# Exact bfloat16 parts for one matrix product, scan states summed on GpSimd, gates by tanh, and filler products of constants on TensorE

## The chip, the core and the metric

The kernel runs on one core of a Trainium2 chip. A core has five engines that each work through their own queue of instructions in order: TensorE (matrix products; PE in the profile, with its weight loads as PEld), VectorE (DVE), ScalarE (ACT), GpSimd (POOL) and SyncE (SP, which issues DMAs here). The metric is the time of one execution on the device in microseconds (us), as the median of several runs.

## The reference, cut to what matters

There are 128 batches of 32 latent rows of 256 numbers, and for each batch a context of 257 rows. Everything is float32. For each batch the reference computes, in this order:

- layer norm, then cross attention of the latents over the raw context, with folded weights, added to the latents;
- a selective scan (a state space block). After a layer norm the rows are projected to 512 channels `x` and 512 channels `delta = relu(...)`. For each of 16 states `s`, `h_t = h_(t-1) * exp(A_s * delta_t) + x_t * delta_t` runs over the 32 rows of a batch; the output of a channel is `sum over s of w_s * h_s`, plus `x * D`, and it is multiplied by a gate, `sigmoid(W_gate * rows + b)`, before the output projection;
- a ternary MLP. `W_fc` holds only -1, 0 and 1: layer norm, 256 to 1024 with gelu, layer norm, 1024 to 256;
- linear attention over the context, whose keys and values are projected by the kernel (relu, cube, norms);
- self attention with a distance decay, 16 heads, over the 32 rows of a batch;
- an MLP with quantized weights and activations.

## The kernel before, in words

Four batches make a group: 128 rows, one row for each partition. There are 32 groups, joined into nine blocks of 2, 4, 4, 4, 4, 4, 4, 4 and 2 groups (`BLOCKS`, line 1442). For each group `context_group` (line 954) loads and transposes the context, does the cross attention, and projects keys and values (`keys`, `keys_values`, products `pkey` and `pval`). For each block `scan_block` (line 1115) does the scan, with the channels in four chunks of 128 partitions and all rows of the block along the free dimension (512 for four groups, 256 for two). For each group `latent_group` (line 1409) then does `mlp` (1171), `linear` (1196), `attention` (1247) and `quantized_mlp` (1379), and stores the rows.

None of this is issued where it is written. A `Recorder` (line 267) takes down every operation with what it reads and writes. `order` (line 384) then puts them in one order, by list scheduling: an estimate of each instruction's duration (`ns_of`, line 42), fixed delays after it (`TAIL`, `HOP`, lines 95 and 96), a due time for each operation that is interpolated within a span of its group (`DUE`, line 1445, one span for each call of `begin`), and constants that weigh the engines against each other (`PRICE`, `WINDOW`, `SOONER`, `AHEAD`, `HORIZON`, lines 554 to 558). It also chooses the engine where an operation may run on two, as `R.relu` and `R.copy` may. `trace` (line 533) issues them; each engine's queue keeps that order strictly. Because all recorded operations are issued by line 540, every row of the profile says L540, and rows are told apart by the names of their tiles.

Buffers are rings: `t1` and `t2` (lines 655 and 658) for intermediate tiles in SBUF, and `bank` (line 578) for the eight PSUM banks.

The places that the change touches:

- `scan_block`. The gate `yg` is a Sigmoid on ScalarE (line 1134). For each chunk, `acc` in PSUM starts as `x * D` (line 1143). For each of 16 states there is an Exp on ScalarE giving `a` (line 1151), a scan on VectorE giving `h` (line 1155), and on VectorE `acc = h * w + acc` (line 1158). Then `acc` is multiplied by the gate (line 1161).
- `mlp`. The rows are transposed by TensorE as they are; the weights `w_fc`, float32, are centred over their inputs once at the start (`centred`, called at line 897), which does the layer norm's subtraction; two halves `ph` of 512 columns are each two float32 products (line 1182).
- `attention`. The latent projection `plat` (line 1260) has its own bank, as has the value projection `pva` (line 1305), which comes after the scores' Exp.

Of the kernel before, what the change touches and what calls it, by code (L numbers as in the profile page):

```python
# [8 lines left out]
F32 = mybir.dt.float32  # L9
# [85 lines left out]
TAIL = {"vector": 75, "scalar": 100, "gpsimd": 25, "tensor": 130, "sync": 0}  # L95
HOP = {"vector": 38, "scalar": 38, "gpsimd": 80, "tensor": 55, "sync": 100}
TABLES = {AF.Exp: "exp", AF.Gelu: "gelu", AF.Sigmoid: "sigmoid"}
# [169 lines left out]
class Recorder:  # L267
# [8 lines left out]
    def together(self):  # L276

        recorder = self

        class Joined:  # L280
            def __enter__(self):
                recorder.joined = []

            def __exit__(self, *_):
                parts, recorder.joined = recorder.joined, None
                ways = {"tensor": ([c for p in parts for c in p[0]], sum(p[1] for p in parts), False)}
                recorder.add(ways, [r for p in parts for r in p[2]], [w for p in parts for w in p[3]])

        return Joined()

    def copy(self, out, in_):
        self.record({"scalar": ("copy", (out, in_), {}), "vector": ("tensor_copy", (out, in_), {})})

# [12 lines left out]
    def begin(self, stage):  # L306

        self.stage = stage
        self.group += 1
        self.spans[self.group] = DUE[self.group]  # L310

    def record(self, calls):
# [33 lines left out]
        if self.joined is not None:  # L346
            self.joined.append((*ways["tensor"][:2], reads, writes))
            return
# [35 lines left out]
    def order(self):  # L384
# [78 lines left out]
        while len(placed) < len(ops):  # L463
# [29 lines left out]
            for k in op.ways:  # L493
                ready[k].remove(i)
            ns = op.ways[e][1]
# [36 lines left out]

    def trace(self, tc):

        last = {}
        for i in self.order():
            op = self.ops[i]
            engine = getattr(self.nc, op.engine)
            for name, args, kw in op.ways[op.engine][0]:
                ins = getattr(engine, name)(  # L540
                    *(traced(a) for a in args), **{k: traced(v) for k, v in kw.items()}
                ).ins
                if op.engine in last:
                    tc.add_manual_dep(
                        ins, last[op.engine].name,
                        mybir.DependencyInfo(
                            mybir.DependencyClass.NoSync, mybir.DependencyReason.DATA
                        ),
                        reason="order",
                    )  # L550
                last[op.engine] = ins


PRICE = {"tensor": 0.0, "vector": 3.195, "scalar": 3.454, "gpsimd": 8.58, "sync": 0.0}
WINDOW = 31.919
SOONER = -0.015
AHEAD = 0
HORIZON = 0.832
# [3 lines left out]
def perceiver_kernel(ctx: ExitStack, tc: tile.TileContext, t: dict, out: bass.AP):  # L562
# [34 lines left out]
    nc.vector.tensor_copy(onesb, ones)  # L597

# [56 lines left out]
    def t2k(shape, name, dtype=F32):  # L655
        return ring("t2", 15).tile(shape, name, dtype)
# [51 lines left out]
    w_fc = wts.tile([P, 2, HID], F32, name="w_fc")  # L708
# [135 lines left out]
    def late_setup():  # L844
        R.vector.tensor_tensor(bd_in, b_in[:, 0:4], d_vec, ALU.mult)
# [51 lines left out]
        centred(w_fc, 2)  # L897
# [142 lines left out]


# [73 lines left out]
    def scan_block(x):  # L1115
        size = len(x)
        tok, batches = size * P, size * GB
# [13 lines left out]
        for ic in range(4):  # L1131
            pg = project(w_gate, ic * P)
            yg.append(t2k([P, TOK], "yg")[:, 0:tok])
            R.scalar.activation(yg[ic], pg, AF.Sigmoid, bias=b_gate[:, ic : ic + 1])
        for ic in range(4):

            dl = t2k([P, TOK], "dl")[:, 0:tok]
            R.scalar.activation(
                dl, project(w_in, DI + ic * P), AF.Relu, bias=b_in[:, 4 + ic : 5 + ic]
            )  # L1140
            xd = project(w_in, ic * P)
            acc = bank("acc")[:, 0:tok]
            R.scalar.activation(
                acc, xd, AF.Identity, bias=bd_in[:, ic : ic + 1], scale=d_vec[:, ic : ic + 1]
            )
            R.vector.scalar_tensor_tensor(xd, xd, b_in[:, ic : ic + 1], dl, ALU.add, ALU.mult)
            dv = dl.rearrange("p (b q) -> p b q", q=LQ)
            for s in range(NST):

                a = a_ring[s % NA][:, 0:batches, :]  # L1150
                R.scalar.activation(
                    a[:, :, 1:LQ], dv[:, :, 1:LQ], AF.Exp, scale=a_neg[:, ic, s : s + 1]
                )
                h = t2k([P, TOK], "h")[:, 0:tok]
                R.vector.tensor_tensor_scan(
                    h, a.rearrange("p b q -> p (b q)"), xd, 0.0, ALU.mult, ALU.add
                )
                R.vector.scalar_tensor_tensor(
                    acc, h, w_st[:, ic, s : s + 1], acc, ALU.mult, ALU.add
                )  # L1160
            R.vector.tensor_tensor(yg[ic], acc, yg[ic], ALU.mult)
# [9 lines left out]
    def mlp(xg):  # L1171

        _, r = stats(xg)
        xT = rows_T(xg)
# [3 lines left out]
        for k in range(2):  # L1178
            ph = bank("ph")
            cols = slice(k * 512, (k + 1) * 512)  # L1180
            with R.together():
                accumulate(ph, [(xT[:, dc, :], w_fc[:, dc, cols]) for dc in range(2)])
            R.scalar.activation(hid[:, cols], ph, AF.Gelu, scale=r)
            R.vector.bn_stats(st[:, k, :], hid[:, cols])
# [62 lines left out]
    def attention(xg):  # L1247
# [3 lines left out]
        with R.together():  # L1251
            for c in range(2):
# [3 lines left out]
                )  # L1256
        qT = t1k([P, D], "qTa").rearrange("p (c n) -> p c n", c=2)
        R.scalar.copy(qT, pq[:, 0:D].rearrange("p (c n) -> p c n", c=2))

        pl_ = bank("plat")  # L1260
        with R.together():
            accumulate(pl_[0:LAT, 0:P], [(wkd[:, dc], xT[:, dc, :]) for dc in range(2)])
        lat = t1k([P, P], "lat")[0:LAT]
        R.scalar.copy(lat, pl_[0:LAT, 0:P])

        pk = bank("pka")
        with R.together():
            for c in range(2):
                accumulate(pk[:, c * P : (c + 1) * P], [(wupk[:, c * P : (c + 1) * P], lat)])
        kd = t2k([P, 2, GB, 2, LQ], "kd")  # L1270
        for r in range(2):
# [3 lines left out]
                scale=odd[:, r : r + 1],  # L1275
            )
# [25 lines left out]

        vd = vds[turn[0] % NV]
        turn[0] += 1
        pv = bank("pva")
        with R.together():
            for b in range(GB):
                for r in range(4):
                    R.tensor.matmul(
                        pv[r * LQ : (r + 1) * LQ, b * 64 : (b + 1) * 64],  # L1310
                        lat[:, b * LQ : (b + 1) * LQ],
                        wupv.rearrange("p (j h k) -> p h j k", h=4, k=16)[:, r],
                        start=True, stop=True,
                    )
        for r in range(4):
            rows_ = slice(r * LQ, (r + 1) * LQ)
            R.scalar.copy(
                vd[rows_, :, :, r, 0:16],
                pv[rows_, 0 : GB * 64].rearrange("p (b j n) -> p b j n", b=GB, j=4),
            )  # L1320
# [88 lines left out]
    def latent_group(xg, kvc, rows_out):  # L1409
        mlp(xg)  # L1410
        linear(xg, kvc)
        attention(xg)
        quantized_mlp(xg)
# [4 lines left out]
    for i, size in enumerate(BLOCKS):  # L1418
# [12 lines left out]
        scan_block(x)  # L1431
# [8 lines left out]
NV = 2  # L1440
PAIR = 2
# [4 lines left out]
    (-1.0, -0.9), (-0.011, 0.566), (-0.809, -0.789), (-0.212, 0.821), (-0.767, 0.109),  # L1446
    (-0.01, 0.15), (0.299, 1.222), (0.556, 1.717), (1.591, 2.698), (1.87, 3.034), (0.619, 0.719),
    (0.863, 0.989), (1.148, 1.233), (1.17, 1.732), (1.498, 2.663), (2.591, 3.75425),
    (2.699, 3.86225), (2.806, 3.97), (2.915, 4.07825), (1.618, 1.802), (1.854, 2.163),
    (2.11, 2.23), (2.365, 2.485), (2.459, 3.663), (3.593, 4.75425), (3.7, 4.86225),  # L1450
    (3.807, 4.97025), (3.915, 5.07825), (2.571, 2.704), (2.985, 3.032), (3.115, 3.236),
    (3.365, 3.485), (3.5, 4.663), (4.591, 5.75425), (4.699, 5.86225), (4.807, 5.97025),
    (4.915, 6.07825), (3.61, 3.735), (3.864, 3.99), (4.115, 4.235), (4.365, 4.431), (4.5, 5.663),
    (5.591, 6.755), (5.699, 6.86225), (5.807, 6.97025), (5.915, 7.113), (4.615, 4.733),
    (4.866, 5.033), (5.115, 5.235), (5.365, 5.485), (5.5, 6.663), (6.612, 7.776), (6.72, 7.884),
    (6.7, 8.26), (6.921, 8.145), (5.616, 5.733), (5.924, 6.173), (6.117, 6.235), (6.462, 6.482),
    (6.501, 7.654), (7.288, 8.301), (7.441, 8.497), (7.544, 8.812), (7.594, 8.984),
    (6.632, 6.743), (6.921, 6.941), (7.171, 7.295), (7.361, 7.611), (7.495, 8.077),
    (7.815, 9.377), (7.667, 9.18), (7.008, 8.283), (7.34, 8.982), (7.658, 7.783), (7.829, 7.849),
    (8.0, 8.585), (8.023, 9.464), (8.392, 9.052),  # L1460
# [78 lines left out]
```

## Time and profile before

| | |
|---|---|
| median of 3 runs | 1765.29 us (1763.37 to 1765.42) |
| the profiled execution | 1760.93 us, of which the span from first to last instruction is 1759.2 us |
| mean granted TensorE clock | 0.973 of full speed |
| TensorE matmul busy | 1660.5 us |
| TensorE weight load busy (beside the products) | 1211.7 us |
| VectorE busy | 1554.4 us |
| ScalarE busy | 1430.8 us |
| GpSimd busy | 1117.0 us |
| table loads on ScalarE | 114, of 1283 ns each |

A row of the profile's groups reads: line, engine, operation, output tile<-input tiles, the shapes, how many; then the busy time of the group in us and the mean duration of one in ns; then the time that the engine stood idle just before them and what ended it. Durations of neighbouring instructions on an engine overlap at their ends, so the busy time of a group is less than count times mean; busy times count a moment once. A float32 matrix product is recorded as two instructions, a bfloat16 product or a transpose as one.

### The profile page before, as it was taken

The page shows a single profiled execution, that of the slowest core. Times are in us where ns is not written, and L with a number is a line of the kernel's source. Part 1 is how long each engine was busy: PE and PEld are TensorE (multiplying, and loading weights), DVE is VectorE, ACT ScalarE, POOL GpSimd, SP SyncE. Part 2 cuts the span into 40 slices and gives each one's busy share as a digit, 9 for nine tenths or more (in the row PEclk, how much of TensorE's full clock was granted, in tenths as well). Part 3 has the DMA queues.
Part 4 walks back from the last instruction along what each step waited for, and adds up shares of the span by engine and source line. Part 5 has one row for each costly group of instructions (what it writes and reads, how often), then busy time and mean ns, then how long its engine had stood idle before and what let it go on. Part 6 is the DMA issues. An engine that isn't in the chain of part 4 may idle for free.

```text
span 1759.2 us, 44923 instructions
## 1 busy us (share of the span) xinstructions
PE 1660.5 (94%) x17268; PEld 1211.7 (69%) x17299; DVE 1554.4 (88%) x3083; ACT 1430.8 (81%) x3442; POOL 1117.0 (63%) x1827
## 2 busy tenths in 40 slices
PE   8999999999999999999999999999999989597886
PEld 6787667766776777766776767766776667366564
DVE  3599799999898999899899999979999999999865
ACT  4587888888788997889788888889888898786655
POOL 5675556744776677666776747865776375347476
PEclk9999999999999999999999999999999999798886
DMA  7221101000110011001100021001100000000000
GB/s 243 74 83 47 61 29 32 29 31 4 48 42 2 16 59 35 29 2 40 41 29 29 7 65 37 29 2 40 40 29 29 1 8 20 4 4 5 5 4 22
DMA packets 44758, 59.69 MB, mean 34 GB/s; under 512 B 8704, under 2 KB 27008, under 8 KB 44544
## 3 DMA queue, kind: packets, MB, share of 16 engines
q1 hardware_dynamic: 44544, 56.81, 10.1%
q8 instruction: 137, 2.24, 0.5%
q14 instruction: 77, 0.63, 0.1%
HBM read 52.32 MB, written 4.19 MB: 32 GB/s over the span
## 4 chain that ended last, share of the span: by engine, by line
PE 75%; DVE 12%; ACT 7%; issue 1%; POOL 1%; DMA 0%; SPq 0%; DVEq 0%; ACTq 0%; POOLq 0%
PE pkey L540 13%; PE pval L540 11%; PE pproj L540 9%; PE pT L540 5%; PE pmlp L540 5%; DVE h L540 5%; PE ph L540 4%; PE pk L540 3%; PE pcT L540 3%; PE pout L540 3%; PE pq L540 3%; DVE acc L540 2%; PE psc L540 2%; PE pqa L540 2%; PE po L540 2%; PE pya L540 2%
## 5 line engine op out<-in xcount | busy, mean ns | idle before, releaser
L540 DVE TENSOR_TENSOR_SCAN h<-a,pproj 128x512 f32<-128x512 f32 (+1 forms) x576 | 617.4, 1087 | 12.4 <-ACT a L540 11.6
L540 ACT ACTIVATE a<-dl,a_neg 128x496 f32<-128x496 f32 (+1 forms) x576 | 369.8, 662 | 60.9 <-DVE h L540 57.6
L540 DVE SCALAR_TENSOR_TENSOR acc<-h,w_st,acc 128x512 f32<-128x512 f32 (+1 forms) x576 | 392.4, 681 | 0.1
L540 PE MATMUL pval<-wkv,cT 128*128 128x256 f32 x1024 | 245.7, 385 | 8.8 <-ACT hid L540 2.3
L540 PE MATMUL pkey<-wkv,cT 128*128 128x256 f32 x1024 | 238.1, 386 | 0.0
L540 POOL TENSOR_TENSOR ku<-ku,e 128x512 f32<-128x512 f32 x128 | 162.1, 1276 | 101.1 <-ACT ku L540 93.3
L540 PEld LDWEIGHTS pval<-wkv,cT 128*128 128x128 f32 x1024 | 189.6, 191 | 44.6 <-issue 7.4
L540 ACT ACTIVATE ks<-ku 128x256 f32<-128x256 f32 x512 | 208.1, 412 | 14.3 <-POOL ku L540 13.1
L540 PEld LDWEIGHTS pkey<-wkv,cT 128*128 128x128 f32 x1024 | 189.3, 190 | 37.7 <-issue 14.5
L540 POOL TENSOR_TENSOR ku<-ks,ku 128x512 f32<-128x512 f32 x128 | 163.7, 1285 | 29.8 <-ACT ks L540 29.1
L540 ACT ACT_TABLE_LOAD x114 | 146.3, 1283 | 5.1 <-PE ph L540 2.5
L540 POOL TENSOR_TENSOR kn<-kn,halves 128x4 f32<-128x4 f32 x128 | 134.1, 1048 | 22.5 <-ACT ks L540 21.7
L540 ACT ACTIVATE vf<-pval,kf 128x256 f32<-128x256 f32 x256 | 107.9, 471 | 40.0 <-PE pval L540 24.5
L540 POOL TENSOR_TENSOR rstd<-rstd,halves 128x1 f32<-128x1 f32 x224 | 123.7, 553 | 15.8
L540 POOL TENSOR_SCALAR rstd<-mv 128x1 f32<-128x1 f32 x224 | 42.9, 192 | 133.7 <-DVE mv L540 110.2
L540 PE MATMUL pproj<-xTs,w_in 128*128 128x512 f32 (+1 forms) x288 | 122.4, 552 | 0.5 <-ACT hT L540 0.2
L540 PE MATMUL ph<-w_fc,xT 128*128 128x512 f32 x256 | 120.2, 597 | 0.6 <-ACT xT L540 0.5
L540 PE MATMUL pmlp<-w_pr,hT 128*128 128x256 f32 x512 | 116.7, 381 | 1.5 <-ACT hT L540 1.2
L540 PEld LDWEIGHTS pmlp<-w_pr,hT 128*128 128x128 f32 x512 | 95.8, 190 | 20.7 <-issue 4.8
L540 ACT ACTIVATION_READ_ACCUMULATOR ks<-ku 128x1 f32 x512 | 99.4, 194 | 0.0
L540 ACT COPY cT<-pcT 128x512 f32<-128x512 f32 x128 | 71.8, 595 | 12.2 <-PE pcT L540 11.8
L540 DVE BATCH_NORM_STATS2 st<-x 128x6 f32<-128x256 f32 x192 | 78.7, 413 | 2.9 <-POOL x L540 1.7
(259 smaller groups left out, 3583.1 us busy)
## 6 DMA issues: line engine op xcount, KB each, us to landing
cx<-in_ctx_dram SPq DMA_DIRECT2D x64, 512.0 KB
x<-in_x_dram SPq DMA_DIRECT2D x32, 128.0 KB
cr<-in_ctx_dram SPq DMA_DIRECT2D x128, 32.0 KB
out_dram<-x SPq DMA_DIRECT2D x32, 128.0 KB
vlz<-vl SPq DMA_DIRECT2D x128, 1.1 KB
w_in<-in_w_inT_dram SPq DMA_DIRECT2D x1, 1024.0 KB
raw_fc<-in_w_fcT_dram SPq DMA_DIRECT2D x2, 512.0 KB
raw_pr<-in_w_prT_dram SPq DMA_DIRECT2D x2, 512.0 KB
```

Source lines behind the costliest of these rows:

```text
L540: ins = getattr(engine, name)(*(traced(a) for a in args), **{k: traced(v) for k, v in kw.items()}).ins
```

## The change

- `mlp`: the row's mean is subtracted first (`xc`, on VectorE or GpSimd as the planner chooses) and the result transposed to `xT`. `xT` is split into three bfloat16 parts `x3` that add up to it: round, subtract, round, subtract. `w_fc` is kept in bfloat16 (its values are -1, 0 and 1) and no longer centred. Each half `ph` is six bfloat16 products (three parts, two chunks of the contraction) in place of two float32 ones.
- `scan_block`: the first 2 states of each chunk (6 in the last two blocks) are multiplied by their weight and added on GpSimd, into a tile `some` in SBUF which starts as `x * D`. The later states go on in `acc` in PSUM on VectorE; the first of them reads `some`.
- The gate: `sigmoid(z) = 0.5 * (1 + tanh(z / 2))`. ScalarE computes tanh, which the planner counts as in the same table as Exp; VectorE computes `(yg + 1) * acc` in one instruction; the half is put into `w_out` at setup.
- `attention`: the latent projection shares the bank of `pqa`, the value projection that of `pka`, and the values are copied ahead of the scores.
- The planner: new `TAIL`, `PRICE` and the other constants, 251 due spans instead of 78 (with `part()`, stages have several), and `t2` has 17 buffers instead of 15.
- `keep_busy`: where the plan has TensorE idle for more than 600 ns ahead of a run that opens a float32 PSUM tile, products of two constant tiles (bfloat16, 512 columns) into that tile are issued first, one for each 216 ns of 0.7 of the gap less 200 ns. The real products then overwrite the tile. In the changed kernel as built there are 172 of them.

```diff
-TAIL = {"vector": 75, "scalar": 100, "gpsimd": 25, "tensor": 130, "sync": 0}
+TAIL = {"vector": 75, "scalar": 90, "gpsimd": 25, "tensor": 215, "sync": 0}
...
-TABLES = {AF.Exp: "exp", AF.Gelu: "gelu", AF.Sigmoid: "sigmoid"}
+TABLES = {AF.Exp: "exp", AF.Gelu: "gelu", AF.Tanh: "exp"}
...
+    def cast(self, out, in_):
+        self.record({
+            "scalar": ("copy", (out, in_), {}), "gpsimd": ("tensor_copy", (out, in_), {}),
+        })
+
+    def minus_column(self, out, in_, column):
+        wide = column.to_broadcast([P, size_of(in_)])
+        self.record({
+            "vector": ("tensor_scalar", (out, in_, column, None, ALU.subtract), {}),
+            "gpsimd": ("tensor_tensor", (out, in_, wide, ALU.subtract), {}),
+        })
...
+    def keep_busy(self, op):
+        out = op.ways["tensor"][0][0][1][0]
+        if min(out.buf.ops) != op.n or out.dtype != F32:
+            return
+        bank = out.buf.traced()[:, 0:512].rearrange("p (a b) -> p a b", a=4)
+        left, right = self.constants
+        for _ in range(int(FILL * (op.gap - 200.0) / 216.0)):
+            self.nc.tensor.matmul(
+                bank, left, right.unsqueeze(1).to_broadcast([P, 4, P]), start=True, stop=True
+            )
...
+            if op.engine == "tensor" and op.gap > GAP:
+                self.keep_busy(op)
...
-PRICE = {"tensor": 0.0, "vector": 3.195, "scalar": 3.454, "gpsimd": 8.58, "sync": 0.0}
-WINDOW = 31.919
-SOONER = -0.015
-AHEAD = 0
-HORIZON = 0.832
+GAP, FILL = 600.0, 0.7
+PRICE = {"tensor": 0.0, "vector": 20.786091, "scalar": 1.959533, "gpsimd": 3.101899, "sync": 0.0}
+WINDOW = 13.816
+SOONER = 0.066
+AHEAD = 0.777235
+HORIZON = 1.581593
...
-        return ring("t2", 15).tile(shape, name, dtype)
+        return ring("t2", 17).tile(shape, name, dtype)
...
-    w_fc = wts.tile([P, 2, HID], F32, name="w_fc")
+    w_fc = wts.tile([P, 2, HID], BF16, name="w_fc")
...
+        R.vector.tensor_scalar(b_gate, b_gate, 0.5, None, ALU.mult)
+        R.vector.tensor_scalar(w_out, w_out, 0.5, None, ALU.mult)
...
-        centred(w_fc, 2)
...
-            R.scalar.activation(yg[ic], pg, AF.Sigmoid, bias=b_gate[:, ic : ic + 1])
+            R.scalar.activation(yg[ic], pg, AF.Tanh, bias=b_gate[:, ic : ic + 1], scale=0.5)
...
-            acc = bank("acc")[:, 0:tok]
+            some = t2k([P, TOK], "some")[:, 0:tok]
...
-                R.vector.scalar_tensor_tensor(
-                    acc, h, w_st[:, ic, s : s + 1], acc, ALU.mult, ALU.add
-                )
-            R.vector.tensor_tensor(yg[ic], acc, yg[ic], ALU.mult)
+                weight = w_st[:, ic, s : s + 1]
+                if s < pooled:
+                    R.gpsimd.tensor_scalar(h, h, weight, 0.0, ALU.mult, ALU.add)
+                    R.gpsimd.tensor_tensor(some, some, h, ALU.add)
+                else:
+                    if s == pooled:
+                        acc = bank("acc")[:, 0:tok]
+                    R.vector.scalar_tensor_tensor(
+                        acc, h, weight, some if s == pooled else acc, ALU.mult, ALU.add
+                    )
+            R.vector.scalar_tensor_tensor(yg[ic], yg[ic], 1.0, acc, ALU.add, ALU.mult)
...
-        _, r = stats(xg)
-        xT = rows_T(xg)
+        mv, r = stats(xg)
+        xc = t1k([P, D], "xc")
+        R.minus_column(xc, xg, mv[:, 0:1])
+        xT = t1k([P, D], "xT")
+        transposed(xc, xT.rearrange("p (c n) -> p c n", c=2), 2)
+
+        x3 = t2k([P, 3, D], "x3", BF16)
+        R.cast(x3[:, 0, :], xT)
+        R.gpsimd.tensor_tensor(xT, xT, x3[:, 0, :], ALU.subtract)
+        R.cast(x3[:, 1, :], xT)
+        R.gpsimd.tensor_tensor(x3[:, 2, :], xT, x3[:, 1, :], ALU.subtract)
...
-                accumulate(ph, [(xT[:, dc, :], w_fc[:, dc, cols]) for dc in range(2)])
+                accumulate(ph, [
+                    (x3[:, k3, dc * P : (dc + 1) * P], w_fc[:, dc, cols])
+                    for dc in range(2) for k3 in range(3)
+                ])
...
+POOLED = 2
+LATE_POOLED = 6
```

## The prediction

> **What bounds the kernel now.** I read the busy time by engine first, then the same by stages, then the chain that ended last, then the groups of instructions.
>
> The stages, from the view of busy time by windows (us; after each busy time its instructions, then the granted clock, the DMA share, GB/s):
>
> ```profile
> core 0: us, PE busy (x) PEld busy (x) DVE busy (x) ACT busy (x) POOL busy (x), PEclk, DMA share, GB/s
> 0.00:100.00 100.00, 90.00 (x813) 69.80 (x814) 51.83 (x133) 52.57 (x168) 63.19 (x108) 0.98 0.48 155
> 100.00:1484.00 1384.00, 1355.35 (x14167) 990.45 (x14189) 1277.14 (x2388) 1190.39 (x2902) 900.22 (x1451) 1.00 0.10 31
> 1484.00:1659.00 175.00, 136.85 (x1527) 97.69 (x1530) 161.82 (x383) 132.65 (x275) 84.14 (x145) 0.87 0.02 4
> 1659.00:1760.00 101.00, 78.34 (x766) 53.75 (x770) 63.64 (x183) 55.17 (x101) 69.45 (x124) 0.79 0.04 12
> ```
>
> Here 1484 is where the last context products (pval) run, and 1659 where the last scan starts. Up to 1484 TensorE is the bound (98% busy, clock 1.00), VectorE close behind (92%). From 1484 to 1659 VectorE is (162 of 175): no contexts are left, the scans of the last two blocks are. After 1659 no engine is full: the last groups' chains of small steps set the time, and the clock is at 0.79. The chain that ended last says so too: PE 75% and DVE 12% of the span.
>
> The groups that the change touches:
>
> ```profile
> L540 DVE SCALAR_TENSOR_TENSOR acc<-h,w_st,acc 128x512 f32<-128x512 f32 x448 | 332.1, 741 | 0.1
> L540 DVE SCALAR_TENSOR_TENSOR acc<-h,w_st,acc 128x256 f32<-128x256 f32 x128 | 60.5, 472 | 0.0
> L540 PE MATMUL ph<-w_fc,xT 128*128 128x512 f32 x256 | 120.2, 597 | 0.6 <-ACT xT L540 0.5 <-DVE hq L540 0.2
> L540 ACT ACT_TABLE_LOAD x114 | 146.3, 1283 | 5.1 <-PE ph L540 2.5 <-PEq L1527 0.8
> L540 POOL TENSOR_TENSOR ku<-ku,e 128x512 f32<-128x512 f32 x128 | 162.1, 1276 | 101.1 <-ACT ku L540 93.3 <-PE pT L540 5.4 <-DVE ku L540 1.4
> L540 POOL TENSOR_SCALAR hq<-hq,qm 128x1024 f32<-128x1024 f32 x32 | 35.7, 1115 | 14.6 <-DVE qm L540 13.7
> L540 POOL TENSOR_TENSOR x<-x,y 128x256 f32<-128x256 f32 x32 | 24.0, 751 | 19.2 <-DVE y L540 18.2 <-PE pval L540 0.8
> ```
>
> To see where each engine's work lies in the new kernel, I gave every instruction of both built orders the duration of its row, scaled to the engine's busy time because means overlap (PE 1660.5 of a sum of 1834.5, DVE 1554.4 of 1770.2, ACT 1430.8 of 1566.2, POOL 1117.0 of 1141.9), and summed by stage.
>
> **The change part by part.**
>
> *TensorE.* The chain shows eight records of ph (four float32 products) in 3.45 us, 0.8625 each, 3.45 us a group. For a warm bfloat16 product of 512 columns the nearest row is phq, the quantized MLP's product, whose timeline has these lines (start, length):
>
> ```profile
> 1487.75 0.38 PE L540 MATMUL phq<-w,qT 128*128 128x512 bf16 x1
> 1492.28 0.59 PE L540 MATMUL phq<-w,qT 128*128 128x512 bf16 x2
> ```
>
> A second one adds 0.21 us. I take 0.216; if they did not overlap it would be the record's 0.38. Twelve a group: 2.59 instead of 3.45, over 32 groups -27.5 us (other end: 12 x 0.38 = 4.56, +35 us; float32 records of 0.39 us also come 0.23 apart, so they overlap). The four pmean<-w_fc products at setup are -3.4. Sum 1660 to about 1629. The 172 products of constants (37 us) lie 59 before the steady stage, 32 in it and 81 after the last pval. The first stage has 10 us of idle TensorE as cover; I charge 4 there, none for the 32 (7 us) where the queue waits anyway.
>
> *VectorE.* 104 accumulations go (72 of 512: 0.741 x 0.878 = 0.65 us; 32 of 256: 0.41): -60. All 21 relus that it did (ku<-pkey, 685 ns) go to ScalarE: -12.6. w_fc's centring less the new halving: -2.7. The gate's product gets 0.06 longer, 36 times: +2. Sum 1554 to 1481.
>
> *ScalarE.* 18 of 114 table loads go (ten ahead of yg, eight in the new order): 18 x 1.283 x 0.914 = -21. Casts +17 (50 of 64 are put here, 0.37 each), relus +11. Sum 1431 to 1438: no gain in time, only in position.
>
> *GpSimd.* A pooled state costs a product by a column (between 403 ns at 256 columns and 1115 at 1024, so 0.64 at 512, 0.40 at 256) and a sum (1.28; 0.74): 72 x 1.92 + 32 x 1.14 = 175. All 32 xc landed here and each group has two subtractions, 96 x 0.73 = 70; 14 casts 5. Sum 1117 to 1361, or 80% of the new time, where it was 63%. In its queue behind these stand rstd, the keys' ku and kn, which ScalarE and then TensorE wait for.
>
> *Port.* A rule of the Trainium skill speaks against this: "SBUF — State Buffer", section "Who interferes with whom", says that GpSimd and a VectorE instruction with two SBUF inputs share a port pair and one waits for the other's whole instruction. The trace shows single cases:
>
> ```profile
> L540 DVE TENSOR_TENSOR wq<-wq,mean x1: 1566/1566/1566, 48.3 to 48.3; 128x512 f32<-128x512 f32 x1
> L540 DVE TENSOR_TENSOR wq<-wq,isp x1: 685/685/685, 44.4 to 44.4; 128x512 f32<-128x512 f32 x1
> L540 DVE TENSOR_TENSOR y<-y,zf x32: 398/416/1546, 269.4 to 1700.4; 128x256 f32<-128x256 f32 x32
> ```
>
> But the median of y<-y,zf is 416, as its neighbour y<-pn,y with a PSUM input (414); the means differ by 43 ns. The scan and acc have one input in PSUM. New with two SBUF inputs are the 36 first accumulations over some. By the rule each could wait 1.28: +46 us of VectorE; by the row 36 x 0.043 = 1.5. I take the row, since such waits are rare here.
>
> *Clock.* "TensorE: Matmul & The Clock Gate", section "What's actually happening", says that an idle window of about 3.4 us halves the clock. The trace has 0.87 and 0.79 after 1484. There TensorE was busy 215 us for what my sums at warm durations put at 194, so 21 us is the most that the 81 fillers can return; if they are late they cost up to 81 x 0.216 = 17.5. I take -4, in the last stage.
>
> *Attention* and t2's two buffers cost and save nothing of their own: same instructions, one PSUM bank less. That is hidden by other groups' products; without cover it is at most the four vd copies of a group (0.37 each).
>
> **Sum by stages.** (1) To the last pval, 1486 us with its run: TensorE's sum there goes from 1463 to 1432, -31; +4 for the first fillers; +5 because in its last four groups the sums are 210 PE, 201 ACT, 203 POOL, 208 DVE, where any delay shows. 1464. (2) To the last scan: VectorE's sum falls from 164 to 111, TensorE's from 131 to 116, GpSimd's becomes about the same. At the old 92% the larger takes 126; I take 130, between that and 145, because three engines are level. (3) After it: 101 us, plus 3.5 for mlp's longer chain (subtraction 0.73, two casts 0.37, two subtractions 0.73, and the mean ahead of the transpose, less 0.9 of TensorE), -4 for the clock, and half of the work that now lies here (VectorE 85 for 62, TensorE 80 for 63): +10. About 110. Span 1464 + 130 + 110 = 1704, where it was 1759.2. The profiled execution took 1760.9 and the median is 1765.3, 6 above the span: 1710.
>
> **The rivals.**
>
> *The tail packs fully.* The work after the last pval is 196 to 199 on PE, DVE and POOL alike; with 10 of loss, 1464 + 207 + 6 = 1677. For it: three engines level and the clock kept. Against: the chain of the last groups, in which no engine is full.
>
> *The tail keeps its length.* If the last chains and not VectorE set it, only stage 1 gains: 1464 + 275 + 6 = 1745. For it: 101 us at 63% of VectorE. Against: the 162 of 175.
>
> *GpSimd takes over: slower.* A pooled pair (1.92 us) stands ahead of ku or rstd in a queue that can't pass it; ScalarE's squares wait, then pval and pk on TensorE. The waits of before, 93 us of POOL for ACT's ku and 110 for DVE's mv, say that it was early and had room; at 80% much of that is gone. The forecast hides all 175 us. If a third (55 us) isn't hidden the gain is gone, and if half isn't, 1710 + 87 = 1797. Against: stage by stage its sum (1168 of 1464) stays under TensorE's by 18%.
>
> *No gain from the parts.* With bfloat16 at 0.38 TensorE would be +35 instead of -27.5: about 1770. Too unlikely by the two lines above for more than a share of "same" or "slower".
>
> **How the numbers follow.** The forecast has 0.62 (own range 1686 to 1734, from stage 2 at 126 to 145 and the port's 46 at a third), the packed tail 0.13, the unshortened tail 0.13, GpSimd or bfloat16 as the new bound 0.12, of which 0.03 end within 0.2%, about what a measurement can tell from no change here. So faster 0.88, same 0.03, slower 0.09. The range 1672 to 1752 holds the packed and the unshortened tail and leaves out 0.2: packing beyond what I see, and GpSimd's case.
>
> **What would show it.** Right: 12 ph records a group at 0.21 apart; 96 table loads; GpSimd busy about 1360 and VectorE 1480; the last pval near 1465; the last scan near 1595; a clock over 0.9 in the tail. Wrong: TensorE idle for kn, ku or rstd in the middle stage (GpSimd), accumulations over some at over 1.5 us (port), fillers that run while their product's input is long there, or the last 100 us become 140.

## The result, and the profile after

The changed kernel takes 1747.26 us (median of four runs, 1742.95 to 1748.23), where the kernel before takes 1764.35 beside it: a ratio of 0.9894, 95% interval 0.9875 to 0.9913. It is faster, by about 17 us and not by the 55 that were forecast. Timed again later, it took 1744.67 (ratio 0.9886, 0.9864 to 0.9907). So two medians of one kernel, taken at different times, lie 2.6 us apart, and differences under some 4 us between runs below are read as nothing.

The profiled span is 1745.6 us (before 1759.2), the mean granted clock 0.987 (0.973). The busy time by stages, cut at the last product pval (1484.8; before 1484.4) and at the start of the last scan (1622.2; before 1658.8), with columns as in the view of before:

```profile
core 0: us, PE busy (x) PEld busy (x) DVE busy (x) ACT busy (x) POOL busy (x), PEclk, DMA share, GB/s
0.00:100.00 100.00, 94.28 (x797) 69.95 (x797) 44.10 (x116) 50.08 (x162) 58.01 (x109) 0.97 0.47 145
100.00:1484.00 1384.00, 1344.38 (x14203) 980.83 (x14259) 1255.47 (x2308) 1195.99 (x2955) 1091.65 (x1680) 1.00 0.10 31
1484.00:1622.00 138.00, 118.94 (x1183) 83.41 (x1186) 120.74 (x280) 102.56 (x226) 110.40 (x188) 0.96 0.01 4
1622.00:1746.00 124.00, 99.73 (x1347) 69.56 (x1354) 87.94 (x254) 78.13 (x155) 96.57 (x171) 0.92 0.04 11
```

The first stage is as long as it was. In its main part (100 to 1484) TensorE and VectorE have less to do than before, and both simply stand idle longer: TensorE 40 us (1384 less 1344.4) where it was 29, VectorE 129 where it was 107. The second stage fell from 174 to 137 us. The third grew from 100 to 123. So by this cut the gain is that of stage 2, less what stage 3 gave back. The cut at the last scan is not a fixed point, though: the new order also puts work behind it that stood ahead of it before (in stage 3 VectorE is busy 87.9 us for 63.6, TensorE 99.7 for 78.3). The two stages together fell from 275 to 261 us.

The groups that the change touches:

```profile
L575 DVE SCALAR_TENSOR_TENSOR acc<-h,w_st,acc 128x512 f32<-128x512 f32 x348 | 257.8, 741 | 0.5
L575 POOL TENSOR_TENSOR ku<-ku,e 128x512 f32<-128x512 f32 x128 | 162.7, 1281 | 33.9 <-ACT ku L575 28.3 <-DVE st L575 5.3
L575 ACT ACT_TABLE_LOAD x95 | 121.9, 1283 | 1.7
L575 POOL TENSOR_TENSOR some<-some,h 128x512 f32<-128x512 f32 x72 | 91.9, 1276 | 2.1
L575 PE MATMUL ph<-w_fc,x 128*128 128x512 bf16 x350 | 89.2, 379 | 5.3 <-ACT ku L575 1.4 <-DVE h L575 0.9 <-POOL x L575 0.7
L575 POOL TENSOR_SCALAR h<-h,w_st 128x512 f32<-128x512 f32 x72 | 50.0, 696 | 27.9 <-DVE h L575 22.8 <-PE pT L575 2.7 <-PE pk L575 1.2
```

Each instruction costs about what the forecast gave it: ph went from 120.2 to 89.2 us, a product by a weight on GpSimd takes 0.696 us (forecast 0.64), a sum 1.276 (1.28). GpSimd as a whole is busy 1356.6 us (forecast 1361). And its wait for ScalarE's ku, 93.3 us before, is down to 28.3: most of the room that it had there is used up.

The chain that ended last, by engine, before and after:

```profile
PE 75%; DVE 12%; ACT 7%; issue 1%; POOL 1%; DMA 0%; SPq 0%; DVEq 0%; ACTq 0%; POOLq 0%
```

```profile
PE 39%; DVE 28%; ACT 14%; POOL 13%; issue 4%; DMA 0%; DVEq 0%; POOLq 0%; ACTq 0%
```

Before, the chain is mostly TensorE's queue. After, it hops between four engines. The experiments below ask why.

### The profile page after: what moved, and what is told of

It reads as the page before. It is cut to its first block, busy times and chain, and to the rows that moved or that the text cites. A ratio compares the mean times of both kernels' runs of the same rounds, so it can differ in the third digit from the quotient of the medians.

```text
span 1745.6 us, 45752 instructions
## 1 busy us (share of the span) xinstructions
PE 1657.3 (95%) x17523; PEld 1203.7 (69%) x17591; DVE 1508.2 (86%) x2956; ACT 1426.8 (82%) x3495; POOL 1356.6 (78%) x2145
## 4 chain that ended last, share of the span: by engine, by line
PE 39%; DVE 28%; ACT 14%; POOL 13%; issue 4%; DMA 0%; DVEq 0%; POOLq 0%; ACTq 0%
DVE h L575 13%; PE pval L575 6%; DVE acc L575 6%; PE pkey L575 6%; PE pproj L575 4%; ACT a L575 3%; PE pT L575 3%; POOL ku L575 2%; POOL rstd L575 2%; ACT ks L575 2%; PE pqa L575 2%; PE pmlp L575 2%; ACT L575 2%; PE pk L575 2%; DVE st L575 2%
## 5 line engine op out<-in xcount | busy, mean ns | idle before, releaser
L575 DVE SCALAR_TENSOR_TENSOR acc<-h,w_st,acc 128x512 f32<-128x512 f32 (+1 forms) x436 | 299.5, 687 | 0.6
L575 POOL TENSOR_TENSOR ku<-ku,e 128x512 f32<-128x512 f32 x128 | 162.7, 1281 | 33.9 <-ACT ku L575 28.3
L575 POOL TENSOR_TENSOR some<-some,h 128x512 f32<-128x512 f32 (+1 forms) x104 | 115.1, 1107 | 2.8
L575 POOL TENSOR_SCALAR h<-h,w_st 128x512 f32<-128x512 f32 (+1 forms) x104 | 65.3, 630 | 40.7 <-DVE h L575 35.5
L575 PE MATMUL ph<-w_fc,x 128*128 128x512 bf16 x350 | 89.2, 379 | 5.3 <-ACT ku L575 1.4
```

What stands on the lines that cost most here:

```text
L575: ins = getattr(engine, name)(*(traced(a) for a in args), **{k: traced(v) for k, v in kw.items()}).ins
```

## The experiments

**Theory.** The queues are in fixed order, and after the change four engines are nearly level (up to 1484: TensorE 97%, VectorE 91%, ScalarE 86%, GpSimd 79% busy). What one of them saves, the others' order doesn't let through, at least in part. **Rivals:** the products of constants delay real ones; GpSimd's added work (or its delays to VectorE) eats the gain; the order that was chosen is at fault; one of the parts of the change is worth nothing.

### The products of constants: e1_no_fillers

```diff
-GAP, FILL = 600.0, 0.7
+GAP, FILL = 1e9, 0.7
```

> The changed kernel in the same order without the 172 products of constants. Theory A (the fillers are hidden: 59 before the steady stage, 32 in it, 81 after the last context products): time within 5 us of 1747, and if anything slower, since the clock falls again in the last 120 us (granted clock there from 0.92 to about 0.8). Theory B (the fillers push the real products behind them, and the missing 22 us of the middle stage are theirs): 15 to 30 us faster, last pval before 1470.

Measured: 1751.23 us, ratio to before 0.9924 (0.9895 to 0.9954), which overlaps the changed kernel's. The windows of this run, same columns:

```profile
1484.00:1622.00 138.00, 109.61 (x1114) 79.74 (x1114) 120.34 (x283) 100.59 (x225) 109.29 (x187) 0.89 0.01 3
1622.00:1746.00 124.00, 98.18 (x1337) 70.03 (x1336) 85.73 (x247) 77.47 (x153) 95.71 (x170) 0.90 0.04 11
```

The fillers do raise the granted clock in stage 2, from 0.89 to 0.96, but the instructions done in each stretch are the same within a few. They neither delay nor speed anything that a measurement can tell. In the last stage the clock is 0.90 without them, and not the 0.8 that was expected: most of its rise from 0.79 is not theirs.

### Relieving one engine at a time

These keep the order of the changed kernel (or of the kernel before) instruction for instruction, and only make some instructions short, so that nothing is planned anew.

```diff
+                if op.tag in SMALL:
+                    args = tuple(
+                        a[:, 0:1] if is_ap(a) and size_of(a) > 1 else a for a in args
+                    )
```

The tag marks, in turn: the pooled states (e2_pooled_small); these and the subtractions for the parts, with a remaining part read twice for the third (e3_gpsimd_light); the odd accumulations on VectorE (e5_vector_light); the odd Exps, on 31 of their 496 or 248 columns (e6_scalar_light).

> The changed kernel in the same order, but each product and sum of a pooled state on GpSimd works on one column of 256 or 512, so that the states left to GpSimd are not summed; GpSimd loses about 140 us, nothing else changes. Theory A (GpSimd's load is what ate TensorE's gain in the middle stage): last pval from 1485 to about 1465, and 25 to 45 us faster in all. Theory B (the middle stage is held by the order of the whole, with waits on every engine): under 12 us faster.

> As the run with pooled states on one column, and also the two subtractions that make the bfloat16 parts on one column, with the third part of the product replaced by a second use of the second: GpSimd loses about 180 us in all and stands near its 1117 of before in load. Theory A (GpSimd): last pval near 1460, 35 to 55 us faster than the changed kernel, near 1700. Theory B: under 15 us faster.

> The changed kernel in the same order, with every accumulation of an odd state after the pooled ones on one column (those states are not summed). VectorE loses about 240 accumulations, some 125 us. Theory C (VectorE's stream sets the changed kernel's middle stage, since neither 55 us of TensorE nor 180 us of GpSimd did): 50 to 100 us faster than 1747. Theory E (four engines are level and hold one another, so that no single one can be relieved to any use): under 20 us faster.

> The changed kernel in the same order, with the Exp of every odd state on one batch of 31 columns instead of 496 or 248 (the other decays of that buffer are left from an earlier state). ScalarE loses about 150 us. Theory C: under 15 us faster. Theory E: under 20 us. A third, D (ScalarE is the bound): 50 to 100 us faster.

TensorE is relieved by computing ph from one part of the three, eight of twelve products fewer (55 us by 256 x 0.216; the cut below is of this run). In the order of before, one of each group's four float32 products of ph is left out (27.6 us), or the accumulations that the change gives to GpSimd run on one column:

```diff
+            if op.tag == "ph":
+                calls = [(n_, a_, {**k_, "start": i == 0, "stop": i == 1}) for i, (n_, a_, k_) in enumerate(calls[::3])]
```

> The changed kernel in the same order with one of the three bfloat16 parts in the product (4 products a group instead of 12, the other parts are made but left out): TensorE loses 32 x 8 x 0.216 = 55 us. Theory A (TensorE no longer bounds the middle stage): under 10 us faster. Theory B (TensorE still bounds it, and waits come on top): 35 to 50 us faster, because about three quarters of the groups do this product before the last context.

> The kernel before in its own order, with one of the four float32 products of ph in each group left out: TensorE loses 32 x 0.8625 = 27.6 us, as much as the bfloat16 parts save. If TensorE bounds the kernel before, as its 98% and its chain of waits say and as the prediction took it: 15 to 25 us faster than before. If it doesn't (each engine waits for the next in a fixed order): under 6 us.

> The kernel before in its own order, with the accumulations of the states that the change gives to GpSimd (2 of 16, 6 in the last two blocks) on one column, so that VectorE loses about 50 us and GpSimd gains nothing. If TensorE bounds the middle stage and VectorE the stretch after it: 25 to 40 us faster, all after the last context products. If VectorE sets the middle stage too: 40 to 55 us faster. If neither: under 10.

Measured. "Busy" is the relieved engine's own busy time in the profile against its kernel's; the gain is between medians, against 1747.26 (changed) or 1764.35 (before); the last column is the engine's share of the chain that ended last in the kernel that was relieved.

| run | relieved | busy, us | time, us (ratio to before, 95%) | gain, us | chain share |
|---|---|---|---|---|---|
| e4_one_part | TensorE | 1657.3 to 1629.4 | 1750.78 (0.9916, 0.9898 to 0.9934) | -4 | 39% |
| e2_pooled_small | GpSimd | 1356.6 to 1220.9 | 1742.20 (0.9869, 0.9848 to 0.9890) | 5 | 13% |
| e3_gpsimd_light | GpSimd | 1356.6 to 1190.4 | 1737.66 (0.9846, 0.9830 to 0.9862) | 10 | 13% |
| e6_scalar_light | ScalarE | 1426.8 to 1341.5 | 1739.63 (0.9861, 0.9842 to 0.9879) | 8 | 14% |
| e5_vector_light | VectorE | 1508.2 to 1410.8 | 1727.27 (0.9794, 0.9776 to 0.9812) | 20 | 28% |
| e7_before_less_ph | TensorE, order of before | 1660.5 to 1645.2 | 1755.99 (0.9958, 0.9937 to 0.9978) | 8 | 75% |
| e8_before_less_acc | VectorE, order of before | 1554.4 to 1514.2 | 1764.52 (1.0000, 0.9984 to 1.0016) | 0 | 12% |

Half or more of each relief is lost. In the changed kernel, 55 us of TensorE's products left out bring nothing, though TensorE is the busiest engine. In part TensorE itself takes them back: its busy time fell by 28 us only, because ph fell from 89.2 to 37.4 us but its other products took longer, at a mean granted clock of 0.979 for 0.987 (in e7, 15 us of 27.6, at 0.969 for 0.973). 166 us less of GpSimd bring 10: it costs something, but isn't what ate the gain. In the order of before, the two savings that the change makes, taken singly, bring 8 (of 27.6 taken out, 15 in busy time) and 0 of 40. None of these seven gave more than the engine's share of the chain times the fall in its busy time (VectorE 28% of 97 is 27, for 20; GpSimd 13% of 166 is 22, for 10; TensorE 75% of 15 is 11, for 8).

Two lines of the order of before, columns as above, say where. In e7, up to its last pval (1477.8):

```profile
100.00:1478.00 1378.00, 1340.20 (x14158) 982.41 (x14179) 1277.74 (x2392) 1191.50 (x2907) 902.05 (x1454) 1.00 0.10 31
```

TensorE has 15 us less to do there than before, and the last pval comes 7 us earlier. In e8, from the last pval (1482.4) to the last scan (1659.3):

```profile
1482.00:1659.00 177.00, 143.11 (x1526) 102.03 (x1528) 154.60 (x382) 131.89 (x274) 84.22 (x145) 0.83 0.01 4
```

VectorE has 7 us less to do than the 161.8 of before, and the stage is no shorter (177 for 174): the granted clock fell from 0.87 to 0.83 and TensorE was busy 143.1 for 136.9. So in that order neither engine was a bound whose savings arrive in full.

Of what had been expected, the theories that named one engine as the bound (B of e4, A of e2 and e3, C of e5, D of e6) all missed. In e5 the 20 us lie at the edge of what theory E allowed; e7's 8 lie between its two cases.

### Relieving three at once: e9_three_light

GpSimd, VectorE and ScalarE lightened together as in e3, e5 and e6.

> The changed kernel in the same order, with three engines relieved together: GpSimd by some 180 us (pooled states and the parts' subtractions on one column, the third part's product a second use of the second), VectorE by some 125 (odd states' accumulations on one column), ScalarE by some 150 (odd states' Exp on 31 columns). TensorE's products are untouched. The three alone gave 10, 20 and 8 us. Theory E (level engines hold one another, so relief shows only where all the others get it): 60 to 120 us faster, last pval before 1462, TensorE then bound. Theory F (the waits are fixed by the order and by the hops between engines, not by load): at most the 40 us of the sum.

Measured: 1711.62 us, 0.9691 (0.9666 to 0.9715): 36 us off, where the single gains sum to 38 (10 + 20 + 8). Its windows, cut at its own last pval (1460.9) and last scan (1589.7), and its chain:

```profile
100.00:1461.00 1361.00, 1342.51 (x14262) 981.67 (x14255) 1162.72 (x2308) 1116.11 (x2955) 958.37 (x1686) 1.00 0.10 32
1461.00:1590.00 129.00, 114.95 (x1184) 81.87 (x1182) 113.70 (x281) 94.62 (x227) 81.63 (x179) 0.99 0.01 4
1590.00:1711.00 121.00, 98.26 (x1354) 69.16 (x1353) 85.71 (x253) 77.74 (x153) 94.43 (x170) 0.93 0.04 12
```

```profile
PE 76%; DVE 10%; ACT 8%; POOL 4%; issue 2%; DVEq 0%; ACTq 0%; POOLq 0%
```

With the other three held at 85%, 82% and 70% of the stage, TensorE is busy 1342.5 of 1361 us (98.6%; before the change 97.9% of 1384) and the last pval comes at 1460.9: 3 us from the 1464 that was forecast from TensorE's sum. So the sum was about right, and it is reached when the others are lightened. Here VectorE had 101 us less to do than in the changed kernel, ScalarE 88 and GpSimd 164.

The size tells something else. Theory E's signs came (the last pval before 1462, TensorE the bound), but its 60 to 120 us did not; theory F's "at most the 40 us of the sum" did. Three reliefs together brought what they bring singly, within the 4 us that count as nothing (by the ratios to before, 36 for 32). So these runs do not show that a relief pays only where the others are relieved too; they show that each passes on a part. TensorE at 98.6% of the stage may have capped what more there was; no run tells.

### Is it the order, or a part of the change?

Three runs took something away and let the order be made anew, with the constants and due times of one of the two kernels. e10_old_planner: the new operations, without fillers, with the delays, constants and 78 spans of before. e11_no_parts: float32 ph as before, no `x3`, ring t2 at 15 (the weights need the space). e12_no_pooled: no states on GpSimd.

```diff
-PRICE = {"tensor": 0.0, "vector": 20.786091, "scalar": 1.959533, "gpsimd": 3.101899, "sync": 0.0}
-WINDOW = 13.816
+PRICE = {"tensor": 0.0, "vector": 3.195, "scalar": 3.454, "gpsimd": 8.58, "sync": 0.0}
+WINDOW = 31.919
```

```diff
-        return ring("t2", 17).tile(shape, name, dtype)
+        return ring("t2", 15).tile(shape, name, dtype)
...
-                accumulate(ph, [
-                    (x3[:, k3, dc * P : (dc + 1) * P], w_fc[:, dc, cols])
-                    for dc in range(2) for k3 in range(3)
-                ])
+                accumulate(ph, [(xT[:, dc, :], w_fc[:, dc, cols]) for dc in range(2)])
```

```diff
-POOLED = 2
-LATE_POOLED = 6
+POOLED = 0
+LATE_POOLED = 0
```

> All operations of the change (parts, pooled states, tanh gates, merged banks), but planned with the constants and 78 due spans of before, without fillers. If the operations bring the gain: 1735 to 1755, as the changed kernel. If the new plan brings it: 1760 to 1790, since the old spans were fitted to other loads.

> The changed kernel with float32 products ph and centred float32 w_fc as before (no parts, no casts, no subtractions; t2 with 15 buffers because of the wider weights), planned anew under the new constants. TensorE gains 31 us of work, GpSimd loses 75, ScalarE 17. If the parts brought what the prediction gave them: 15 to 30 us slower than 1747. If a lighter GpSimd and a shorter chain at the end are worth as much: within 8 us of it.

> The changed kernel with no state on GpSimd (all 16 accumulated on VectorE), planned anew under the new constants: VectorE +60 us of work, GpSimd -175. If pooled states gave the 38 us that the stretch after the last context products lost: 25 to 45 us slower than 1747. If the relief of VectorE is worth nothing, as in the order of before: within 8 us.

Measured: 1964.94 us (1.1126, 1.1101 to 1.1150), 1812.42 (1.0268, 1.0240 to 1.0295) and 1864.12 (1.0550, 1.0520 to 1.0580). Read as the worth of a part these would be absurd: all are slower than the kernel before. A fourth run changed nothing but ring t2, from 17 to 15:

> The changed kernel with one number altered: ring t2 has 15 buffers, as before the change, and not 17. Every operation, constant and due time of the changed kernel stays; only the order that results is another. Theory (the order is fitted to one set of loads and buffers, and any step off it costs tens of us): 1790 to 1830 us, as in the run without parts (1812), which had 15 buffers too; what that run showed would then be the buffers and the unfitted order and not the parts. Rival (the parts are what that run had lost): 1745 to 1760 here.

It took 1830.32 us (1.0372, 1.0331 to 1.0412): 83 us more with the same operations, constants and due times. The constants fit one set of loads and buffers, and off it the order falls apart. The three runs above missed both of their expectations by 30 us or more; e13 lies at the upper edge of its theory. So those three tell of the fit at least as much as of the parts, and each part had to be taken away again with constants and due times searched anew for what is left (the operations are those of e11_no_parts, of e12_no_pooled, and, in the third, states on GpSimd in the last two blocks alone):

```diff
-POOLED = 2
+POOLED = 0
```

> The changed kernel without the bfloat16 parts (float32 ph, centred w_fc, ring t2 15), and with the constants and due times fitted anew to this set of operations by a search over several hundred orders. TensorE has about 30 us more, GpSimd some 75 less. Theory (TensorE's relief alone does not reach the end, as with one part in three, which gained nothing for 55 us): 1750 to 1770, at or below the kernel before. Rival (the parts bring the 31 us that the forecast's first stage had): 1775 or more.

> The changed kernel with all states accumulated on VectorE (no states on GpSimd), constants and due times fitted anew by the same search. VectorE has about 64 us more, GpSimd 175 less. Theory (VectorE's relief is what the change lives on, 20 us for 125 in the lightened run and 38 in stage 2): 1765 to 1785, no faster than the kernel before. Rival (GpSimd's load takes back what VectorE gives, so pooling is worth nothing): 1740 to 1755.

> The changed kernel with states on GpSimd in the last two blocks alone (6 of 16 each, as in the change; none in the first seven, where the change has 2), constants and due times fitted anew by the same search. Theory (in the stage up to the last pval the relief of VectorE does not reach the end, so only the late states count): 1745 to 1757, within 10 of the changed kernel. Rival (the early states carry the gain): at 1765 or above.

Measured: 1760.74 us (0.9976, 0.9960 to 0.9993) without parts, 1767.38 (1.0009, 0.9990 to 1.0027) without pooled states, 1746.42 (0.9894, 0.9862 to 0.9927) with late states alone. The busy times, in this order:

```profile
PE 1684.0 (96%) x17439; PEld 1212.9 (69%) x17474; DVE 1503.6 (85%) x2960; ACT 1427.9 (81%) x3459; POOL 1294.1 (74%) x2035
```

```profile
PE 1670.5 (95%) x17588; PEld 1207.3 (68%) x17655; DVE 1548.6 (88%) x3076; ACT 1429.6 (81%) x3500; POOL 1171.0 (66%) x1918
```

```profile
PE 1658.3 (95%) x17556; PEld 1202.2 (69%) x17623; DVE 1524.5 (87%) x3012; ACT 1427.1 (82%) x3499; POOL 1250.0 (72%) x2029
```

All three lie in the range of their theory. What they say:

- Parts without pooled states (but with the tanh and all else) gain nothing (1767 against 1765); pooled states without parts gain 4 to 5; both together gain 17 to 19. It looks as if only both together count. But the four times belong to four orders, each with a search of its own, and in one and the same order three reliefs simply added up (e9). So that the two halves need each other is not shown; searches of unequal success would look the same.
- The early states bring nothing. With 48 accumulations of 512 columns and 8 of 256 put back on VectorE (48 x 0.65 + 8 x 0.41 = 34 us by the forecast's prices, 16 in its busy time), the time is the changed kernel's.
- The late ones carry the rest, between these two orders: with 24 of 512 and 24 of 256 columns taken from VectorE in the last two blocks (25 us by the same prices, 24 in its busy time), the time falls from 1767 to 1746.

Where these 21 us arrive is less plain. The stages of e15 (last pval 1519.1, last scan 1656.4) and of e16 (1509.3 and 1621.5), columns as above:

```profile
1519.00:1656.00 137.00, 121.18 (x1205) 85.86 (x1212) 129.31 (x340) 106.53 (x235) 82.95 (x147) 0.98 0.01 4
1656.00:1766.00 110.00, 90.05 (x1289) 62.92 (x1292) 76.69 (x226) 74.32 (x146) 87.88 (x152) 0.95 0.04 13
```

```profile
1509.00:1622.00 113.00, 104.42 (x1097) 77.13 (x1100) 105.64 (x263) 94.22 (x214) 96.99 (x168) 0.98 0.01 3
1622.00:1744.00 122.00, 101.99 (x1403) 69.16 (x1409) 87.83 (x258) 77.03 (x157) 99.58 (x175) 0.97 0.04 13
```

Ten of them come ahead of the last pval; stage 2 is 25 shorter and stage 3 is 13 longer. VectorE was the fullest engine of e15's stage 2 (94%), with TensorE at 88%. And e15, without any pooled state, has a stage 2 of 137 us, as the changed kernel has; it loses its time ahead of it. So each order spreads its time over the stages in its own way, and only the whole times compare.

The fitted orders are each less worked on than the changed kernel's, so the worth of a part read from them is an upper bound. The order with late states alone was searched on for longer (e17), and timed beside the changed kernel:

> The run with states on GpSimd in the last two blocks alone, its constants and due times searched on for as long again (an order that keeps the layer norm's and the keys' waits apart otherwise is not forced; the operations are the same). Theory (the early states on GpSimd give nothing, so an order fitted as closely as the changed kernel's does as well or a little better): 1738 to 1746. Rival (the early states do give something which the closer fit of the changed kernel shows): 1747 or more, above the changed kernel beside it.

> The changed kernel unaltered, beside the run above and on the same chip, for a ratio between the two: 1743 to 1749, as it was.

1744.33 us (0.9880, 0.9857 to 0.9903) and 1744.67 (0.9886, 0.9864 to 0.9907): the same. The early states can go and nothing is lost; no order was found that beats the changed kernel's.

## Why the prediction was wrong in size

**The step that failed** is in the sum by stages: "(1) To the last pval, 1486 us with its run: TensorE's sum there goes from 1463 to 1432, -31; +4 for the first fillers; +5 because in its last four groups the sums are 210 PE, 201 ACT, 203 POOL, 208 DVE". It took a TensorE busy at 98% for a bound whose savings arrive in full, and charged 5 us for the others being level. The stage gave 0 of the 22 it promised. The sum itself was right: e9_three_light has its last pval at 1460.9, and in e1_no_fillers TensorE is busy 1428 us up to the last pval, for the 1432 of the forecast. What was wrong is that the stage would shorten with the sum while VectorE stands at 91%, ScalarE at 86% and GpSimd at 79% of it. Even in the order of before, with GpSimd's load unchanged, a relief of TensorE alone brought the last pval forward by 7 us of 15 (e7). The forecast noted the levels for the last four groups; they hold for the whole stage.

The whole shortfall of the span, 1745.6 for 1704, is 21 us in stage 1 (1484.8 for 1464), 7 in stage 2 (137.4 for 130) and 13 in stage 3 (123.4 for 110).

**The instruction prices** held. Bfloat16 products: six of a group's half in one row of the timeline (start, length),

```profile
1400.45 1.46 PE L575 MATMUL ph<-w_fc,x 128*128 128x512 bf16 x6
```

that is 0.216 each after the first 0.38, as taken from phq. Table loads: 96, as forecast (95 in the row above, one at another line). GpSimd: 1356.6 for 1361. ScalarE: 1426.8 for 1438. VectorE came to 1508.2 and not 1481; some 17 of the 27 us are waits that lengthen its instructions, below.

**Stage 2** came out nearly in size, 37 us shorter for 45, but its mechanism is not shown. The forecast let the stage follow VectorE's sum. In the order of before, taking VectorE's accumulations away did not shorten it (e8), and e15 has as short a stage without a pooled state. That the late states are worth up to 21 us is shown for the whole time, not for this stage; that the number of the stage agrees may be luck.

**Stage 3** was mis-sized. "Half of the work that now lies here: +10": the stage is 23 us longer, about as much as the work that came into it (TensorE has 99.7 us after the last scan for 78.3, VectorE 87.9 for 63.6). That the whole of this work counts is a reading; no run takes it out. The clock did rise, from 0.79 to 0.92, but e1 has 0.90 there without fillers, and a stage as long within 2 us, so little of the -4 that the forecast gave them is theirs. It isn't GpSimd's added work: in e3_gpsimd_light the last scan starts at 1614.2 and the stage is still 120 us.

**The port.** The forecast weighed the Trainium skill's rule ("SBUF — State Buffer", section "Who interferes with whom") for the 36 accumulations over `some` alone and took 1.5 us, by the row. These 36 did get longer, but by little: 28 of 512 columns took 829 ns for their neighbours' 741, which is 2.5 us, and 8 of 256 columns 672 for 474, 1.6 us; and y<-y,zf went from a mean of 450 to 529 ns, 32 times, 2.5 us. It missed who else waits. The group of the normed rows, before and after:

```profile
L540 DVE TENSOR_SCALAR xn<-x,mv,rstd 128x256 f32<-128x256 f32 x96 | 41.2, 439 | 10.6 <-POOL rstd L540 10.5
```

```profile
L575 DVE TENSOR_SCALAR xn<-x,mv,rstd 128x256 f32<-128x256 f32 x96 | 52.4, 552 | 18.4 <-POOL rstd L575 12.2 <-PE pka L575 5.9 <-ACT ls L575 0.2
```

96 x 0.113 is 11 us, with a median that stays at 407 ns (405 before): a few long ones make it, 18 over 0.6 us for 7 before (minimum, median and maximum in ns, before and after):

```profile
L540 DVE TENSOR_SCALAR xn<-x,mv,rstd x96: 360/405/1439, 54.4 to 1736.7; 128x256 f32<-128x256 f32 x96
```

```profile
L575 DVE TENSOR_SCALAR xn<-x,mv,rstd x96: 320/407/2298, 50.7 to 1719.5; 128x256 f32<-128x256 f32 x96
```

The longest, in the timeline of the changed kernel (start, length):

```profile
699.64 0.24 POOL L575 COPY vf<-kf 128x32 f32<-128x32 f32 x1
699.73 2.30 DVE L575 TENSOR_SCALAR xn<-x,mv,rstd 128x256 f32<-128x256 f32 x1 [1.43 <-POOL rstd L575]
699.81 2.06 POOL L575 TENSOR_TENSOR kvx<-kvc,band 128x1088 f32<-128x1088 f32 x1
```

The subtraction ends at 702.03, 0.16 us after GpSimd's instruction of 2.06 us does. It is no chance: all 18 long ones end 0.146 to 0.154 us after a GpSimd instruction, as do the 7 of before; of the 78 short ones only 12 end 0.13 to 0.17 us after one. So they wait for GpSimd. The same section counts `tensor_scalar` among the operations that can enter a mode of two ports and then contend with GpSimd; the forecast used only the case of two SBUF inputs. Whether this one is in that mode no run here shows. A mean by instruction hides such waits and a maximum shows them. How much depends on the order rather than on how much GpSimd does: with 136 us less of it in the same order (e2_pooled_small) the mean is still 532 ns.

**The rivals.** "GpSimd takes over" is not what happened: lightening it by more than half of what was added brings 10 us. "The tail keeps its length" named 1745, close to the measurement, but by the opposite road: it had the first stage gain 22 and the tail keep its 275 us, where the first stage gained nothing and the tail fell to 261. That the time agrees is no support for its reasons.

**What stays open.** The runs show that level engines in fixed queues pass on only part of a relief; they don't show which single waits hand it from one engine to the next. In the main part of stage 1 VectorE's largest wait is for ScalarE's `some` (36.7 us in nine waits, where it was 21.0 for `acc` before), while TensorE's 40 idle us are spread thin, 4.4 us at most for one pair of tiles; no run removes either. The share of the 23 us in stage 3 that another order could take back wasn't found. And no run has the old operations under a newly searched order, or the changed kernel without the tanh gates or the shared banks: what order, gates and banks give by themselves isn't known, but e15, which has them all and the parts, is no faster than the kernel before.

## What to carry to other kernels

A stage in which one engine is at 97% and another at 91% has no single bound: a relief of one engine does not arrive at its full price. In the seven reliefs that kept the order, the engine's share of the chain that ended last, times the fall in its busy time, bounded the gain from above. Between orders that are searched anew it does not: from e15 to e16 21 of 24 us came through, where VectorE's share of e15's chain was 34%. And where an order is fitted to its loads, taking a part away without fitting it again measures the fit as well: two ring buffers fewer cost 83 us here, more than any part of the change was worth.

## What the runs showed of the hardware that was not expected

- A VectorE `tensor_scalar` with one SBUF tensor and two column operands can last 2.30 us where its median is 0.407, ending with the GpSimd instruction beside it; all 18 that took over 0.6 us end about 0.15 us after a GpSimd instruction. Over the 96 of them the cost was 11 us more than before.
- With products of TensorE left out, its other products took longer: 55 us less of them lowered its busy time by 28, at a mean granted clock of 0.979 for 0.987.
- Products of constants on an idle TensorE raised the granted clock of a stage from 0.89 to 0.96 and left the time as it was within what can be measured.
